# In the run of y's products, the second batch's first product is cut in two pieces, two columns at its old place and 128 columns at the end of the run

## The chip, the core and the metric

The kernel runs on one core of one Trainium2 chip. The core has a matrix engine (TensorE, PE in the profile, with its weight loads shown as PEld), a vector engine (VectorE, DVE), a scalar engine (ScalarE, ACT), a general engine (GpSimd, POOL), and queues that issue DMA transfers. The engines run side by side, each works through its own list of instructions in order, and they wait for each other by semaphores. The metric is the device time of one execution in microseconds, the lower the better.

## What is computed

Twelve layers of linear attention (there is no softmax) over a batch of 16 sequences of 256 tokens with 128 features, then a layer norm, a gated feed-forward block and another layer norm. The core of the reference, one layer with 16 heads of 8 features:

```python
for i in range(N_LAYER):
    qkv = x @ Wqkv[i].T + bqkv[i]
    q, k, v = jnp.split(qkv, 3, axis=-1)          # each (B, H, T, D) after a reshape
    att = jnp.einsum('bhqd,bhkd->bhqk', q, k) * scale
    y = jnp.einsum('bhqk,bhkd->bhqd', att, v)
    x = y @ Wproj[i].T + bproj[i] + x             # y with the heads side by side again
...
x = _layernorm(x0 + x)
h = jax.nn.silu(x @ wg.T) * (x @ wu.T)
x = _layernorm(x + h @ wd.T)
```

## The kernel before

Since nothing between the token vectors and the attention is nonlinear, the kernel doesn't carry tokens through the twelve layers. For each sequence it carries a matrix of 128 features by 130 columns (`tst`): the 128x128 map from the first tokens to the present ones, a column (number C = 128) for the share that all tokens have in common, and one column of padding. So W = C + 2 = 130. The tokens come in as a 128x128 Gram matrix of the first tokens for each sequence (`g0`). In each layer a sequence needs: q, k and v's maps from the state (`products`, L434 to L448), the Gram matrix times v (L455), the 8x8 blocks of k times that for each head (`mm_m` in `heads`, L499), these blocks times q (`mm_y`, L517, the run of y), and the projection with the sum into the state (`projection`, L534 to L541).

Sequences go in pairs (PB = 2, eight pairs p), and four pairs make a set (G = 4, two sets o). A call of `heads` treats one layer and one set: 8 sequences. The heads' blocks lie on the diagonal, so the 128x128 product falls into four groups of 32 features (four heads each), `group(g)`. TensorE's array is used there in tiles of 32 rows by 32 columns. In the run of y, the product of pair r, group g and sequence b takes rows `group(g)` of the weights `gm` and of q, and writes columns of the array `group(g + r)`, which are partitions of the output, into pair r's own bank of the accumulation memory, columns b W to (b + 1) W. So the 16 combinations of r and g use the 16 tiles of the array once each, all for the first sequence of the pairs (b = 0, the first batch); then all again for the second (b = 1). "First tile" is that of r = 0 and g = 0. There are 24 such runs (12 layers by 2 sets), each of 32 products. The data is fp32, and TensorE takes such a product in two passes with a weight load each: the profile shows 64 loads and 64 matmuls a run, not 32.

Behind the run of y, each pair's bank is rounded to the type fp32r (`yh`, on ACT or DVE by the copy helper, L205 or L207), DVE subtracts this from the bank to get the rest (`yl`, L530), and the projection multiplies both (L534 to L536: the low weights with yh, the high weights with yh and with yl). Pair r's projection waits for bank r alone. Its q is written by L444's matmuls, a copy (tile `qgv`) and a small addition to column C (L448); the first loads of the run of y wait for those.

The order of all work is settled when the program is built. Each `plan.op` has the estimated cost on each engine that could do it, what it reads and writes, and a priority; `Plan.run` places one operation after another, picks the engine that would end it first, and writes the instructions out in that order. A run of y is one operation with an estimate of 1200 ns on PE, whatever order its products have inside. TensorE's own list behind a run of y goes on with other pairs' products, which don't depend on it (L434 to L436, then L455), and reaches the projections about 2 us later.

The line at the core of the run, before:

```python
for b in range(PB):
    for r, p in enumerate(pairs):
        for g in range(G):
            nc.tensor.matmul(bank(pys[r])[group(g + r), b * W : (b + 1) * W], gm[group(g), r * PB + b, :], qss[p][group(g), b, :], start=True, stop=True)
```

Of the kernel before, what the change touches and what calls it, by code (L numbers as in the profile page):

```python
# [21 lines left out]
C = 128  # L22
# [3 lines left out]
PB = 2  # L26
NP = B // PB
W = C + 2
# [8 lines left out]
G = 4  # L37
# [141 lines left out]
def dve(n, fast=False):  # L179
    return 69 + n / (1.92 if fast else 0.96)  # L180


def pool(n):
    return 147 + 2.1 * n
# [7 lines left out]
def linear_attention_ffn_kernel(ctx: ExitStack, tc: tile.TileContext, x, xt, wall, wq0, bias, wg, wu, wd, out):  # L192
    nc = tc.nc
# [7 lines left out]
    bank = lambda v: banks[v.slot]  # L201
# [10 lines left out]
    def mul(e, dst, a, b):  # L212
        (nc.vector if e == DVE else nc.gpsimd).tensor_tensor(dst, a, b, ALU.mult)  # L213
# [104 lines left out]
    qss = [t[:, : PB * W].rearrange("p (a b) -> p a b", b=W) for t in qgvs]  # L318
# [52 lines left out]
    def offset_products(l, o):  # L371

        raw, pc = wts[l][0], Val("bank")
        c = tst[:, o * OB : (o + 1) * OB, C]

        def mm():
            for s in range(1 if l else 0, 3):
                for g in range(G):
                    cols = slice(32 * g, 32 * g + 32)
                    nc.tensor.matmul(bank(pc)[cols, s * OB : (s + 1) * OB], wraw[raw.slot][:, s * C : (s + 1) * C][:, cols], c, start=True, stop=True)  # L380
        return [raw, *vc[o * G : (o + 1) * G]], pc, mm

    def offsets(l, o, prio, pc):


        bs, ps = slice(o * OB, (o + 1) * OB), slice(o * G, (o + 1) * G)
        c = tst[:, bs, C]
        step = lambda costs, f, reads, writes: plan.op(costs, f, reads, writes, prio)
        src = lambda s: bank(pc)[:, s * OB : (s + 1) * OB]
        step({DVE: 133}, lambda e: nc.vector.tensor_scalar(vb[:, bs], src(2), bcol[:, l, 2:3], None, ALU.add), [pc, vbias], [vvc[o]])  # L390
        step({DVE: 133}, lambda e: nc.vector.tensor_scalar(kb[:, bs], src(1), bcol[:, l, 1:2], float(T), ALU.add, ALU.mult), [pc, vbias], [vkb[o]])
        if l == 0:
            step({DVE: 133}, lambda e: nc.vector.tensor_scalar(qc[:, bs], src(0), bcol[:, 0, 0:1], None, ALU.add), [pc, vbias], [vqc[o]])
        step({DVE: dve(32 * OB)}, lambda e: nc.vector.transpose(flat(vbb[:, bs]), vb[:, bs].unsqueeze(2).to_broadcast([128, OB, 32])), [vvc[o]], [vvb[o]])
        step({DVE: dve(32 * OB)}, lambda e: mul(e, kvo[:, bs], vbb[:, bs], kb[:, bs].unsqueeze(2).to_broadcast([128, OB, 32])), [vvb[o], vkb[o]], [vkvo[o]])

        if l < L - 1:
            def share(e):
                if e == ACT:
                    nc.scalar.activation(c, c, AF.Identity, bias=bcol[:, l, 3:4])  # L400
                else:
                    nc.gpsimd.tensor_scalar(c, c, bcol[:, l, 3:4], 0.0, ALU.add, ALU.add)
            step({POOL: 200, ACT: 220}, share, [vbias, *(vhi[ps] if l else [])], vc[ps])
# [68 lines left out]
    def first_offsets(o, prio):  # L472
        def fill(e):
            for p in range(o * G, (o + 1) * G):
                nc.gpsimd.tensor_copy(qss[p][:, :, C], qc[:, p * PB : (p + 1) * PB])
        plan.op({POOL: 600}, fill, [vqc[o]], vqo[o * G : (o + 1) * G], prio)

    def heads(l, o, prio, riders):

        raw = wts[l][0]
        pairs = range(o * G, (o + 1) * G)
        gm = gms[o]
        pm, pys = Val("bank"), [Val("bank") for _ in pairs]
        group = lambda g: slice(32 * (g % G), 32 * (g % G) + 32)
        src = [raw] if l == 0 else [vkv[p] for p in pairs]

        more = [(*r, *offset_products(*r)) for r in riders]

        def mm_m(e):
            for _, _, _, _, mm in more:
                mm()
            for p in pairs:
                for b in range(PB):
                    n = (p - o * G) * PB + b
                    tk = wraw[raw.slot][:, C : 2 * C] if l == 0 else kvs[p][:, b, 0, :]
                    for g in range(G):
                        nc.tensor.matmul(bank(pm)[group(g), n * 32 : n * 32 + 32], tk[:, group(g)], gvs[p][:, b, group(g)], start=True, stop=True)  # L499
        reads = [v for _, _, rs, _, _ in more for v in rs]  # L500
        if l == 0 and o == 1:

            reads += vw[:G]
        plan.op({PE: 890 + 140 * len(more)}, mm_m, [*(vgv[p] for p in pairs), *src, *reads], [pm, *(m[3] for m in more)], prio)
        for lo, oo, _, pc, _ in more:
            offsets(lo, oo, prio + (OFFSET if lo else 0), pc)
            if lo == 0:
                first_offsets(o, prio)
        plan.op({DVE: dve(OB * 32)}, lambda e: nc.vector.tensor_tensor(
            gm, bank(pm)[:, : OB * 32].rearrange("p (b j) -> p b j", j=32), kvo[:, o * OB : (o + 1) * OB], ALU.add), [pm, vkvo[o]], [vgm[o]], prio)  # L510
        plan.op({DVE: dve(OB * 32), POOL: pool(OB * 32)}, lambda e: mul(e, gm, gm, mask32.unsqueeze(1).to_broadcast([128, OB, 32])), [], [vgm[o]], prio)

        def mm_y(e):
            for b in range(PB):
                for r, p in enumerate(pairs):
                    for g in range(G):
                        nc.tensor.matmul(bank(pys[r])[group(g + r), b * W : (b + 1) * W], gm[group(g), r * PB + b, :], qss[p][group(g), b, :], start=True, stop=True)  # L517
        plan.op({PE: 1200}, mm_y, [vgm[o], *(vq[p] for p in pairs), *(vqo[p] for p in pairs)], pys, prio)
        return pys

# [231 lines left out]
    for l in range(L):  # L752
        if l + 1 < L:
            prep_weights(l + 1)
        for o in range(NO):
            at = l + OSTEP * o
            for p in range(o * G, (o + 1) * G):
                products(l, p, at)
            for r, py in enumerate(heads(l, o, at, [(l, o)] * (l < OWN) + [(l + o, 1 - o)] * (OWN <= l + o < L))):
                projection(l, o * G + r, py, at + (LSTEP * r if l == L - 1 else 0))  # L760
        if l < NP:
            center_tokens(l, l + 2)
# [38 lines left out]
```

## Time and profile before

| | |
|---|---|
| median of 3 runs | 305.56 us (304.95 to 306.38) |
| the profiled execution | 305.16 us, of which the span is 303.2 us |
| instructions | 12834 |
| granted TensorE clock | 0.998 of full speed |
| TensorE matmuls busy | 294.3 us (97% of the span) |
| TensorE weight loads busy | 269.8 us (89%) |
| DVE, ACT, POOL busy | 226.1, 217.7, 137.8 us |
| y's matmuls (L517) | 1536, 280 ns mean, 25.8 us together |
| y's weight loads | 1536, 103 ns mean, 17.2 us together |

The span is the time from the first to the last instruction that the profiler recorded; the difference to the execution's own time lies before and behind it. Durations of instructions on one engine can overlap, so that a sum of means is not time: 64 matmuls of 280 ns of one run of y stand in 1.07 us. Starts are what counts there. A line such as "102.98 1.07 PE L517 MATMUL ... x64" of the timeline gives the start in the span, the time covered, the engine, the line of the kernel, what is done and how often. In a bracket behind it stands how long the engine was idle before, and what ended the wait. "Issue" there means that the profile shows nothing that was waited for.

### The profile page before, as it was taken

The page shows a single profiled execution, that of the slowest core. Times are in us where ns is not written, and L with a number is a line of the kernel's source. Part 1 is how long each engine was busy: PE and PEld are TensorE (multiplying, and loading weights), DVE is VectorE, ACT ScalarE, POOL GpSimd, SP SyncE. Part 2 cuts the span into 40 slices and gives each one's busy share as a digit, 9 for nine tenths or more (in the row PEclk, how much of TensorE's full clock was granted, in tenths as well). Part 3 has the DMA queues.
Part 4 walks back from the last instruction along what each step waited for, and adds up shares of the span by engine and source line. Part 5 has one row for each costly group of instructions (what it writes and reads, how often), then busy time and mean ns, then how long its engine had stood idle before and what let it go on. Part 6 is the DMA issues. An engine that isn't in the chain of part 4 may idle for free.

```text
span 303.2 us, 12834 instructions
## 1 busy us (share of the span) xinstructions
PE 294.3 (97%) x5376; PEld 269.8 (89%) x5376; DVE 226.1 (75%) x683; ACT 217.7 (72%) x559; POOL 137.8 (45%) x208
## 2 busy tenths in 40 slices
PE   8999999999999999999999999999999999999981
PEld 8989999999999999999999999989999998878760
DVE  4796887777677676876767777786644789999993
ACT  3556877867777768777686666777887558788875
POOL 8256452334531445225432354224431167777883
PEclk9999999999999999999999999999999999999999
DMA  7624213112031120311302102120000000000225
GB/s 214 163 91 131 67 39 89 38 46 82 3 89 37 39 89 4 88 40 28 98 2 56 37 17 50 49 68 17 2 2 4 3 1 2 0 0 8 63 70 138
DMA packets 22489, 15.65 MB, mean 52 GB/s; under 512 B 1952, under 2 KB 19872, under 8 KB 22432
## 3 DMA queue, kind: packets, MB, share of 16 engines
q1 hardware_dynamic: 21872, 14.62, 17.3%
q8 instruction: 42, 0.69, 0.9%
q10 hardware_dynamic: 560, 0.22, 0.3%
q14 instruction: 15, 0.12, 0.1%
HBM read 8.02 MB, written 2.10 MB: 33 GB/s over the span
## 4 chain that ended last, share of the span: by engine, by line
PE 87%; DVE 10%; issue 1%; ACT 1%; POOLq 0%; POOL 0%; DVEq 0%
PE bank L455 14%; PE bank L434 8%; PE bank L517 8%; PE bank L436 7%; PE bank L435 7%; PE bank L442 5%; PE bank L499 5%; PE bank L536 4%; PE bank L534 4%; PE bank L535 4%; PE bank L443 3%; PE bank L444 3%; PE bank L336 3%; DVE st L618 2%; PE bank L706 2%; PE bank L707 2%
## 5 line engine op out<-in xcount | busy, mean ns | idle before, releaser
L210 POOL TENSOR_TENSOR thl<-tst,thl 128x260 fp32r<-128x260 f32 x88 | 64.8, 768 | 123.1 <-ACT thl L205 123.1
L205 ACT COPY qgv<-bank 128x256 f32<-128x256 f32 x169 | 59.8, 378 | 19.2 <-PE bank L444 12.9
L205 ACT COPY kv<-bank 128x512 f32<-128x512 f32 (+1 forms) x93 | 53.4, 575 | 19.5 <-PE bank L436 14.2
L434 PE MATMUL bank<-whl,thl 128*128 128x256 f32 x176 | 51.9, 295 | 0.0
L436 PE MATMUL bank<-whl,thl 128*128 128x256 f32 x176 | 49.7, 282 | 0.0
L435 PE MATMUL bank<-whl,thl 128*128 128x256 f32 x176 | 49.4, 281 | 0.0
L455 PE MATMUL bank<-kv,g 128*128 128x128 f32 x352 | 46.1, 275 | 0.0
L541 DVE TENSOR_TENSOR tst<-bank,tst 128x260 f32<-128x260 f32 x96 | 36.9, 425 | 9.4 <-PE bank L536 9.0
L205 ACT CAST thl<-tst 128x260 fp32r<-128x260 f32 x88 | 33.0, 408 | 14.6 <-DVE tst L541 14.5
L455 PEld LDWEIGHTS bank<-kv,g 128*128 128x128 f32 x352 | 42.7, 191 | 0.4 <-issue 0.4
L448 DVE TENSOR_SCALAR qgv<-bank,bcol 128x2 f32<-128x2 f32 x88 | 19.2, 221 | 28.3 <-ACT qgv L205 22.9
L434 PEld LDWEIGHTS bank<-whl,thl 128*128 128x128 f32 x176 | 33.1, 188 | 4.0 <-issue 3.8
L530 DVE TENSOR_TENSOR yhl<-bank,yhl 128x260 fp32r<-128x260 f32 x96 | 34.4, 420 | 2.2 <-ACT yhl L205 2.1
L436 PEld LDWEIGHTS bank<-whl,thl 128*128 128x128 f32 x176 | 33.1, 188 | 0.3 <-POOL thl L210 0.2
L435 PEld LDWEIGHTS bank<-whl,thl 128*128 128x128 f32 x176 | 33.2, 189 | 0.0
L442 PE MATMUL bank<-thl,whl 128*128 128x260 f32 x88 | 28.8, 327 | 0.0
L205 ACT CAST yhl<-bank 128x260 fp32r<-128x260 f32 (+1 forms) x61 | 21.8, 408 | 8.3 <-PE bank L517 7.7
L207 DVE CAST yhl<-bank 128x260 fp32r<-128x260 f32 (+1 forms) x43 | 16.7, 430 | 12.7 <-PE bank L517 12.7
L517 PE MATMUL bank<-qgv,gm 32*32 32x130 f32 x1536 | 25.8, 280 | 0.2 <-DVE gm L213 0.2
L443 PE MATMUL bank<-thl,whl 128*128 128x260 f32 x88 | 24.8, 282 | 0.0
L444 PE MATMUL bank<-thl,whl 128*128 128x260 f32 x88 | 24.7, 281 | 0.0
L517 PEld LDWEIGHTS bank<-qgv,gm 32*32 32x32 f32 x1536 | 17.2, 103 | 5.5 <-ACT kv L205 0.3
(157 smaller groups left out, 694.7 us busy)
## 6 DMA issues: line engine op xcount, KB each, us to landing
wraw<-wall SPq DMA_DIRECT2D x12, 256.0 KB, 3.0
wpt<-whl SPq DMA_DIRECT2D x24, 96.0 KB, 2.2
qgv<-x SPq DMA_DIRECT2D x8, 256.0 KB, 5.0
xt<-xt SPq DMA_DIRECT2D x8, 256.0 KB, 3.1
out<-kv SPq DMA_DIRECT2D x7, 256.0 KB, 2.3
wpt<-whl SPq DMA_DIRECT2D x24, 64.0 KB, 2.7
wpt<-whl SPq DMA_DIRECT2D x24, 32.0 KB, 1.9
wraw<-wg SPq DMA_DIRECT2D x1, 192.0 KB, 3.2
```

The costliest lines, as they stand in the source:

```text
L205: nc.scalar.copy(dst, src)
L210: (nc.vector if e == DVE else nc.gpsimd).tensor_tensor(dst, a, b, ALU.subtract)
L434: nc.tensor.matmul(o, hi[:, b, 0:C], hl(0, 1, 2), start=True, stop=False)
L435: nc.tensor.matmul(o, hi[:, b, 0:C], hl(1, 1, 2), start=False, stop=False)
L436: nc.tensor.matmul(o, lo[:, b, 0:C], hl(0, 1, 2), start=False, stop=True)
L442: nc.tensor.matmul(o, hl(0, 0), flat(hi), start=True, stop=False)
L443: nc.tensor.matmul(o, hl(0, 0), flat(lo), start=False, stop=False)
L444: nc.tensor.matmul(o, hl(1, 0), flat(hi), start=False, stop=True)
L455: nc.tensor.matmul(bank(pgv)[:, b * C : (b + 1) * C], g0[p][:, b, :], tv(b), start=True, stop=True)
L517: nc.tensor.matmul(bank(pys[r])[group(g + r), b * W : (b + 1) * W], gm[group(g), r * PB + b, :], qss[p][group(g), b, :], start=True, stop= ...
L530: plan.op({DVE: dve(PB * W)}, lambda e: nc.vector.tensor_tensor(yl, bank(py)[:, : PB * W], yh.bitcast(F32), ALU.subtract), [py, vyh[p]], [ ...
L541: plan.op({DVE: dve(PB * W)}, lambda e: nc.vector.tensor_tensor(ts, bank(pw)[:, : PB * W], ts, ALU.add), [pw], [vt[p], vc[p]], prio)
```

## The change

The first batch's 16 products stay as they are. Of the second batch, the first tile's product (r = 0, g = 0) is cut along the columns that stream through the array: its last two columns, 128 and 129, are done at its old place, between the two batches, and its columns 0 to 127 behind the fifteen other products, as the last thing of the run. Both pieces use the same weights, which are loaded for each. A run has 33 products then in place of 32, and the last writer of pair 0's bank is the last product of the run. Nothing else is changed; the operation's estimated cost is the same.

```diff
+        tiles = [(r, g) for r in range(G) for g in range(G)]
+        order = [(0, r, g, 0, W) for r, g in tiles]
+        for b in range(1, PB):
+            order += [(b, 0, 0, C, W), *((b, r, g, 0, W) for r, g in tiles[1:]), (b, 0, 0, 0, C)]
+
         def mm_y(e):
-            for b in range(PB):
-                for r, p in enumerate(pairs):
-                    for g in range(G):
-                        nc.tensor.matmul(bank(pys[r])[group(g + r), b * W : (b + 1) * W], gm[group(g), r * PB + b, :], qss[p][group(g), b, :], start=True, stop=True)
+            for b, r, g, lo, hi in order:
+                nc.tensor.matmul(bank(pys[r])[group(g + r), b * W + lo : b * W + hi], gm[group(g), r * PB + b, :], qss[pairs[r]][group(g), b, lo:hi], start=True, stop=True)
         plan.op({PE: 1200}, mm_y, [vgm[o], *(vq[p] for p in pairs), *(vqo[p] for p in pairs)], pys, prio)
```

## The prediction

> **What bounds the kernel now.** I read the page first: its engine rows, the slices, then the chain of the work that ended last.
>
> ```profile
> PE 294.3 (97%) x5376; PEld 269.8 (89%) x5376; DVE 226.1 (75%) x683; ACT 217.7 (72%) x559; POOL 137.8 (45%) x208
> ...
> PEclk9999999999999999999999999999999999999999
> ...
> PE 87%; DVE 10%; issue 1%; ACT 1%; POOLq 0%; POOL 0%; DVEq 0%
> ```
>
> TensorE is busy for 97% of the span at its full clock (0.998 granted), and 87% of the chain is TensorE's. So a nanosecond more or less in a y run is a nanosecond of the end, if TensorE does not wait for data just behind it. Next I read the chain in order of time around one y run, and the weight loads there:
>
> ```profile
> 103.05 1.00 PE bank L517 x56
> ...
> 102.97 0.80 PEld L517 LDWEIGHTS bank<-qgv,gm 32*32 32x32 f32 x64
> 103.98 0.19 PEld L434 LDWEIGHTS bank<-whl,thl 128*128 128x128 f32 x1 [0.20 <-issue]
> ```
>
> The reader is to see that the y run stands whole on the chain, with 0.20 us behind its last matmul in which the array changes from 32x32 tiles to 128x128. One product is four records: two weight loads and two passes, 64 of each in a run. There are 24 runs. Then I cut the run into stretches (columns: us, PE busy, PEld busy with their counts, clock, DMA):
>
> ```profile
> 102.97:103.22 0.25, 0.24 (x32) 0.24 (x33) 1.00 0.00 0
> 103.22:103.29 0.07, 0.07 (x32) 0.00 (x0) 1.00 0.40 110
> 103.29:103.41 0.12, 0.12 (x30) 0.10 (x1) 1.00 0.86 213
> 103.41:103.78 0.37, 0.37 (x42) 0.36 (x30) 1.00 0.69 176
> 103.78:103.98 0.20, 0.20 (x25) 0.00 (x0) 1.00 0.15 36
> ```
>
> This is the place the change touches. The first batch loads its 32 weights and the first one of the second batch (33), then nothing is loaded for 0.07 us, then one weight in 0.12 us, then 30 in 0.37 us. Start by start in the trace, from the run's first load (102.97): first passes of batch one at 2 to 102 ns, one each 6.7 ns; second passes at 137 to 237; the second batch's first product passes at 322 and 433; its second product loads at 437; from there one product each 16.6 ns, to a last pass at 807; the next load, L434's, at 1004. The second batch's first product therefore seems to hold up the other fifteen.
>
> **What holds it.** The question is whether that product is held by its own length (the tile streams 130 columns twice, and pass two cannot start before pass one is through: 322 + 108 = 430), or by something that doesn't depend on it. The trace has a second case: the runs of m (L499, behind L380's), whose passes are short, so that no tile is busy for long. There too, products come fast at first, and then on a grid of 16.6 ns. What sets the start of this grid is the same to a nanosecond in all: it is the recorded end of the second pass of the run's very first product, plus 30 to 31 ns. In the usual y run that pass starts at 137 and lasts 269, to 406, and the load of the 18th product is at 437. In the runs of m behind L380 it ends at 230 and the load is at 260. In the one m run that stands alone, at 233 us, it ends at 251 and the load is at 282. The 17th product's first pass obeys it too: the first product's first pass ends at 295, the 17th's starts 27 later, at 322; its second pass starts 27 after 406, at 433. In the y run at 200.6 us, whose first product came late, the same ends are 298 and 409, and the starts 324 and 435. So it looks as if 16 products (64 records) may be open, and the 17th gets in record by record as the first one ends. This is my reading of these rows; it says that the 17th product's length is not what the others wait for.
>
> **The change part by part.** Removed: the 17th product as one of 130 columns. Put in its place: two columns of it, four records again. By the reading above they get in when the first batch's first product ends, as now: passes at 322 and 433, next load at 437. Gain: nothing. The bounds: at worst nothing is lost, since the records are as many; at best the two passes follow each other at the nearest short row. In the m runs behind L380, passes of 8 and of 32 columns on one tile follow each other at 31 to 32 ns alike, so 433 would be 353: 80 ns a run, 24 x 80 = 1.9 us. I take nothing, because the m runs, whose passes are short, are held to the same end.
>
> Added: at the end, four records on the tile of row 0 and column 0, 128 columns. That tile's load is free from 237 on, and rows and columns of tiles go on in the order that the run had. On the grid it costs one step: 16.6 ns (its passes would start at about 690 and 823). The last pass streams 128 columns in place of 130, less by 2 x 108/130 = 1.7 ns, before the 197 ns from the last pass to L434's load. Net: +15 ns a run, 24 x 15 = +0.36 us. Bounds: with the step hidden altogether, -1.7 x 24 = -0.04 us. If the piece were to run alone, as the 17th product does now (322 to 441), 119 - 1.7 = 117 ns, 24 x 117 = +2.8 us. I take the grid, whose fifteen steps stand directly ahead of it and include changes of row, column and bank.
>
> [...] The trace puts a whole product, two loads and two passes, on 16.6 ns here, so its row goes into the sum.
>
> Moved: the signal that bank 0 is ready. At present the four banks of the run are announced at 0.89, 0.98, 1.08 and 1.17 us from its start, 92 ns apart. Bank 0's last writer goes from the 20th product of the run to the very end, behind bank 3's; by the same spacing its signal comes at about 1.19, some 0.3 us later. ACT (in some runs DVE) has the rounding of that bank to yhl first in its queue and the next banks' behind it. What covers it, by the timelines of ACT, DVE and TensorE:
>
> ```profile
> 103.89 0.66 ACT L205 CAST yhl<-bank 128x260 fp32r<-128x260 f32 x2 [0.22 <-PE bank L517]
> 105.01 0.59 ACT L205 COPY kv<-bank 128x512 f32<-128x512 f32 x1 [0.47 <-PE bank L436]
> ...
> 104.66 1.42 DVE L530 TENSOR_TENSOR yhl<-bank,yhl 128x260 fp32r<-128x260 f32 x4
> 106.59 0.43 DVE L541 TENSOR_TENSOR tst<-bank,tst 128x260 f32<-128x260 f32 x1 [0.50 <-PE bank L536]
> ...
> 105.88 0.36 PE L534 MATMUL bank<-yhl,whl 128*128 128x260 f32 x1
> ...
> 106.20 0.28 PE L536 MATMUL bank<-yhl,whl 128*128 128x260 f32 x1
> ```
>
> ACT's two roundings move 0.3 us into the 0.47 us in which it idles for L436. DVE's first subtraction (L530, 104.66) is behind DVE's own roundings, and TensorE needs its result at 106.20, 1.1 us after its end at 105.08. In the runs where DVE rounds banks 0 and 1, the four subtractions come 0.3 us later and 0.9 us are left. The thin places are the first run (0.05 us at L536, but DVE's own roundings set it, not bank 0's) and the last two, with 0.56 and 0.40 us. Priced at nothing; if that cover were gone in these three, 3 x 0.3 = +0.9 us. What is late next in that case is L536 of the first projection. The order of the operations, their engines and all DMA queues stay as they are: the planner's costs are untouched. The waits on q's copies stand on the first batch's loads and cover both batches.
>
> Sum: the profiled execution took 305.16 (span 303.2, 1.96 around it), which becomes 305.52. It lies 0.40 under the median of 305.56; against that the forecast is 305.56 + 0.36 = 305.9.
>
> **Rivals.** First, the 17th product's own length is what holds the others. For it: 322 + 108 is 430, as near to 433 as the other reading's sum. Against it: the m runs. The time: -80 + 15 = -65 ns a run, -1.6 us, 304.0 (beyond 0.5% by a hair). Second, slower: the last piece runs alone at the end of each run, its passes one after the other with nothing beside them, 117 ns a run, 308.4. For it: the run's other product on this tile that has an open stretch to itself took 111 between its passes. Against it: the grid lets the first passes of products run ahead of earlier second passes. It decides from 64 ns a run, where 24 runs make 1.53 us (0.5%). Third, the late bank 0 reaches TensorE at the thin places: 305.9 + 0.9 = 306.8.
>
> **How the numbers follow.** A measurement of this kernel tells about 0.5% (1.5 us) from no change. Forecast 72%, its own range 305.2 to 306.7 from the spread of the runs shown (-0.6 to +0.8 around the median). First rival 10%, two thirds of it beyond 0.5%; second 9%; third 9%, a small part of it beyond. Faster 7%, within 0.5% 83%, slower 10%. The range takes in the forecast, the third rival and the near edge of the first: 304.5 to 306.9.
>
> **What would show it.** In the profile after: 66 loads and 66 passes in each y run; passes of the two-column piece at about 322 and 433; the next load at 437; the last pass near 823, L434's load near 1019; bank 0's rounding 0.3 us later and no new wait at L534 and L536. I am wrong if the two-column passes stand 30 ns apart and the next load comes well ahead of 437, or if the last product's passes are followed by a longer pause than 197 ns.

## The result, and the profile after

The changed kernel takes 306.48 us (median of 20 runs, 305.38 to 307.64) against 305.59 us for the kernel before (20 runs, 304.77 to 307.35). The ratio is 1.003, with a 95% interval of 1.0016 to 1.0044: 0.5 to 1.35 us slower, around 0.9. That lies inside the range that was given (304.5 to 306.9) and within the 0.5% that was called the likeliest. The amount was put at 0.36 us, below the interval's lower end.

The page of the changed kernel, in the lines that were shown of before, and two of its list of DMA queues that are needed further on (packets, MB, share of 16 engines):

```profile
PE 295.2 (97%) x5424; PEld 270.5 (89%) x5424; DVE 226.5 (74%) x683; ACT 217.4 (71%) x559; POOL 137.7 (45%) x208
...
PEclk9999999999999999999999999999999999999998
...
q8 instruction: 42, 0.69, 1.0%
q14 instruction: 14, 0.11, 0.1%
...
PE 87%; DVE 10%; issue 1%; ACT 1%; POOLq 0%; POOL 0%; DVEq 0%
```

There are 48 loads and 48 passes more (two of each in 24 runs), TensorE is busy 0.9 us longer, and its share of the chain is what it was. The bound has not moved to another engine. The span is 304.1 us (303.2 before).

The chain in order of time, around the same run of y (start, us, what):

```profile
103.84 1.02 PE bank L522 x53
104.86 0.32 PE bank L434
```

The weight loads there (start, us, line and operation, how many, idle before):

```profile
103.77 0.82 PEld L522 LDWEIGHTS bank<-qgv,gm 32*32 32x32 f32 x66
104.79 0.19 PEld L434 LDWEIGHTS bank<-whl,thl 128*128 128x128 f32 x1 [0.20 <-issue]
```

And the run cut into stretches at the same offsets as before (stretch, us, PE busy with its count, PEld busy with its count, clock, DMA share, GB/s):

```profile
103.77:104.02 0.25, 0.25 (x32) 0.24 (x33) 1.00 0.00 0
104.02:104.09 0.07, 0.07 (x32) 0.00 (x0) 1.00 0.39 110
104.09:104.21 0.12, 0.12 (x30) 0.10 (x2) 1.00 0.83 205
104.21:104.59 0.38, 0.38 (x43) 0.38 (x32) 1.00 0.86 217
104.59:104.79 0.20, 0.20 (x26) 0.00 (x0) 1.00 0.15 36
```

The reader is to see that the pattern has not changed. The first batch loads its 32 weights and the first of the second batch, then nothing for 0.07 us, then two weights in 0.12 us, then 32. Start by start from the run's first load: the two-column passes at 323 and 434, the next load at 438, the last pass at 823, L434's load at 1019 (1004 before). It is 1018 or 1019 in 19 of the 24 runs. The 20th run, whose first product comes late, takes 1037, against 1023 before: the same step. The forecast had 322, 433, 437, 823 and 1019.

Bank 0's rounding and what hangs on it, by the timeline of ACT:

```profile
104.95 0.65 ACT L205 CAST yhl<-bank 128x260 fp32r<-128x260 f32 x2 [0.49 <-PE bank L522]
105.81 0.59 ACT L205 COPY kv<-bank 128x512 f32<-128x512 f32 x1 [0.20 <-PE bank L436]
```

and by that of DVE:

```profile
105.43 1.42 DVE L535 TENSOR_TENSOR yhl<-bank,yhl 128x260 fp32r<-128x260 f32 x4
107.40 0.43 DVE L546 TENSOR_TENSOR tst<-bank,tst 128x260 f32<-128x260 f32 x1 [0.55 <-PE bank L541]
```

The rounding starts 1.18 us behind the run's first load (0.92 before; bank 0's signal was put at 1.19), and ACT's idle time ahead of L436's copy has shrunk from 0.47 to 0.20 us, as foretold. L539 and L541 (L534 and L536 of before) show no new wait in any run. One thing about the signals was not foreseen: TensorE raises its semaphore three times at the end of a run of y, at 0.96, 1.12 and 1.16 us, where it did so four times before (0.89, 0.98, 1.08, 1.17). In three of the 24 runs it does so once.

So the run of y does what was forecast, within about a nanosecond, in 20 runs of 24. The other four hold the rest. The longest of them, by the weight loads and by the chain:

```profile
83.76 0.72 PEld L522 LDWEIGHTS bank<-qgv,gm 32*32 32x32 f32 x55
84.94 0.17 PEld L522 LDWEIGHTS bank<-qgv,gm 32*32 32x32 f32 x11 [0.46 <-issue]
85.30 0.19 PEld L434 LDWEIGHTS bank<-whl,thl 128*128 128x128 f32 x1 [0.20 <-issue]
```

```profile
83.83 0.92 PE bank L522 x47
84.75 0.19 issue
84.94 0.43 PE bank L522 x11
```

Behind its 55th load this run, the eighth, stands still: 0.46 us without a load, of which 0.19 us is seen on the chain as a time in which TensorE had nothing to do and waited for nothing that the profile names. Its next load of L434 comes at 1545 ns in place of 1019. The others are the 11th run (1083), the 14th (1066) and the 12th (1027). Summed over the 24 runs, the time from the first load to L434's load is 988 ns more than before: 360 ns of added steps (24 x 15) and 628 ns of such holds. Not all of it stays to the end: between the runs of y the profile gains 0.33 us, which is taken up below.

**What stands at the holds.** I counted TensorE's records (loads, passes and its semaphore records) from the start of its list. The load at which a hold ends is number 3521 in this run, and 4801 and 6082 in the 11th and 14th: the remainder against 256 is 193 or 194. The queue q8 above carries 42 packets of 16 KB; 42 x 256 = 10752 is the number of TensorE's loads and passes in the kernel before, and in `eight` below it carries 45 for 11520, which is 45 x 256. So I put a packet at 256 records. The hold ends 1.34 to 1.50 us behind the end of such a transfer: in the eighth run the transfer lasts from 82.14 to 83.47, and the load comes at 84.94. In the kernel before, the smallest distance from a transfer's end to the load at this place is 1.32 us, in the 16th run, with no hold. So it looks as if TensorE ran out of instructions: the next block of its list had not become usable yet. That is my reading of these rows; what they show is the remainder and, in this run, 0.46 us without a load. Four more records a run move all later boundaries (28 records by the eighth run), and some fall late into a run of y, where the kernel before starts 128 records in 0.81 us, against 3.6 us in the mean of its list (10752 in 303.2 us).

### The profile page after: what moved, and what is told of

Its sections match the earlier page's. It is cut to its first block, busy times and chain, and to the rows that moved or that the text cites. A ratio compares the mean times of both kernels' runs of the same rounds, so it can differ in the third digit from the quotient of the medians.

```text
span 304.1 us, 12908 instructions
## 1 busy us (share of the span) xinstructions
PE 295.2 (97%) x5424; PEld 270.5 (89%) x5424; DVE 226.5 (74%) x683; ACT 217.4 (71%) x559; POOL 137.7 (45%) x208
## 4 chain that ended last, share of the span: by engine, by line
PE 87%; DVE 10%; issue 1%; ACT 1%; POOLq 0%; POOL 0%; DVEq 0%
PE bank L455 14%; PE bank L522 8%; PE bank L434 8%; PE bank L436 7%; PE bank L435 7%; PE bank L442 5%; PE bank L499 5%; PE bank L539 4%; PE bank L541 4%; PE bank L540 4%; PE bank L444 3%; PE bank L443 3%; PE bank L336 3%; DVE st L623 2%; PE bank L711 2%; PE bank L712 2%
## 5 line engine op out<-in xcount | busy, mean ns | idle before, releaser
L434 PE MATMUL bank<-whl,thl 128*128 128x256 f32 x176 | 51.8, 294 | 0.0
L436 PE MATMUL bank<-whl,thl 128*128 128x256 f32 x176 | 49.4, 281 | 0.0
L434 PEld LDWEIGHTS bank<-whl,thl 128*128 128x128 f32 x176 | 33.1, 188 | 3.9 <-issue 3.8
L436 PEld LDWEIGHTS bank<-whl,thl 128*128 128x128 f32 x176 | 33.1, 188 | 0.3 <-POOL thl L210 0.2
L522 PE MATMUL bank<-qgv,gm 32*32 32x130 f32 (+2 forms) x1584 | 26.6, 277 | 0.4 <-issue 0.2
```

Of the source, the lines that this page charges most:

```text
L434: nc.tensor.matmul(o, hi[:, b, 0:C], hl(0, 1, 2), start=True, stop=False)
L436: nc.tensor.matmul(o, lo[:, b, 0:C], hl(0, 1, 2), start=False, stop=True)
L522: nc.tensor.matmul(bank(pys[r])[group(g + r), b * W + lo : b * W + hi], gm[group(g), r * PB + b, :], qss[pairs[r]][group(g), b, lo:hi], st ...
```

## The experiments

Two theories of the 0.9 us were tried against each other. The first is that of the prediction with the holds added: 0.36 us of steps, and what the shifted instruction list costs. The second is the prediction's third rival in a wider form: the moved last writer of bank 0 costs something somewhere. Ahead of the experiments the reading of the queue (16 products open, the 17th gets in as the first ends) was open as well. All edits below are against the changed kernel unless it is said otherwise. In the table, the run's length is the time from the first load of a run of y to L434's load, in the middle one of 24 runs; "steps" and "held" divide what the 24 runs of one profile sum to above those of the kernel before: the middle run's excess 24 times, and the rest. What is held need not be held at a boundary of the list.

| kernel | ratio, 95% interval | run, ns | steps, ns | held, ns |
|---|---|---|---|---|
| changed | 1.0030 [1.0016, 1.0044] | 1019 | 360 | 628 |
| again | 1.0029 [1.0016, 1.0043] | 1019 | 360 | 960 |
| whole_last | 1.0002 [0.9989, 1.0015] | 1005 | 21 | 0 |
| swap | 1.0023 [1.0007, 1.0039] | 1005 | 24 | 934 |
| in_place | 1.0013 [1.0000, 1.0027] | 1021 | 408 | 224 |
| first_short | 1.0035 [1.0019, 1.0051] | 1009 | 120 | 215 |
| eight | 1.0110 [1.0086, 1.0133] | 1135 | 3144 | 269 |
| before_s28 | 1.0018 [1.0003, 1.0032] | 1004 | 0 | 11 |
| before_s28_2 | 1.0008 [0.9996, 1.0019] | 1004 | 0 | 0 |
| swap_s44 | 0.9997 [0.9981, 1.0013] | 1005 | 8 | 0 |
| whole_last_s28 | 1.0009 [0.9992, 1.0026] | 1004 | 0 | 305 |
| after_s44 | 1.0031 [1.0018, 1.0045] | 1017 | 312 | 50 |
| after_s44_2 | 1.0033 [1.0020, 1.0045] | 1017 | 312 | 98 |

**again.** The changed kernel without an edit, for a second profile.

> The changed kernel once more, nothing edited. Three theories of its +0.9 us. The step: the added product costs one step of 16.6 ns less 1.7, 24 runs make +0.36 us, ratio 1.0012, and what goes beyond is not the change's. Held supply: with four more records a run, TensorE's list of instructions falls otherwise into the pieces in which it is fetched, and single runs are held in the middle; in the profile after, the run at 83.8 us is held 0.53 us, and three others 0.12 us together. Then the hold comes back at the same run, and the ratio is again near 1.003. Accident: holds come in each execution at other places or not at all; then this profile has them elsewhere or has none, and over many executions the ratio goes toward 1.001.

The middle run is 1019 again, and the eighth run is held at the same load:

```profile
83.56 0.72 PEld L522 LDWEIGHTS bank<-qgv,gm 32*32 32x32 f32 x55
84.69 0.17 PEld L522 LDWEIGHTS bank<-qgv,gm 32*32 32x32 f32 x11 [0.41 <-issue]
```

The 11th run is held longer than in the first profile (1371 against 1083), the 14th too (1111). In the fifth, load 2241, again with remainder 193, is held by 0.05 us without making the run longer. So these places belong to the program, and the length of a hold differs from one execution to another. The 18th run (1076) is held as well, at load 7773, whose remainder is 93. It is held at the same number in `in_place` (1130), and by 0.05 us in after_s44 and after_s44_2 at 7817, the same load of the program with the list 44 records longer ahead of it. That hold doesn't go with the blocks of the list, and nothing here shows what makes it; the fourth run of `eight` (1267, remainder 178) has another.

**whole_last.** The product is not cut, but done whole at the end of the run.

```diff
-            order += [(b, 0, 0, C, W), *((b, r, g, 0, W) for r, g in tiles[1:]), (b, 0, 0, 0, C)]
+            order += [*((b, r, g, 0, W) for r, g in tiles[1:]), (b, 0, 0, 0, W)]
```

> The second batch's first product isn't cut but goes whole to the end of the run (32 products, the moved signal of bank 0 stays). The step: nothing is added, so the run is as long as before (last pass at 807, next load at 1004) and the ratio 1.000 (0.999 to 1.001); the product that is now the 17th is another one of 130 columns, and its passes are at 322 and 433 too. Were the late signal of bank 0 what costs, this kernel would keep the whole +0.9 us, 1.003. Held supply: as many records as before, so 1.000.

```profile
102.60 0.80 PEld L522 LDWEIGHTS bank<-qgv,gm 32*32 32x32 f32 x64
103.60 0.19 PEld L434 LDWEIGHTS bank<-whl,thl 128*128 128x128 f32 x1 [0.20 <-issue]
```

With 64 loads the run takes 1005, nothing is held, and the time is that of before (1.0002). Bank 0's signal is late here as in the changed kernel, and the run raises three signals as there. So the lateness by itself doesn't bring the 0.9 us (the interval leaves it 0.46 at most). The 17th place is taken by another tile's product of 130 columns, and its passes start at 322 and 433 as ever. With the two-column piece's 323 and 434 this shows that neither the length nor the tile of the 17th product sets them.

**swap.** The pieces change places: 128 columns at the old place, two at the end.

```diff
-            order += [(b, 0, 0, C, W), *((b, r, g, 0, W) for r, g in tiles[1:]), (b, 0, 0, 0, C)]
+            order += [(b, 0, 0, 0, C), *((b, r, g, 0, W) for r, g in tiles[1:]), (b, 0, 0, C, W)]
```

> The two pieces change places: 128 columns as the 17th product, two columns at the end. As many products and records as in the changed kernel. The step: the last piece streams so briefly (passes near 690 and 746) that the 32nd product's second pass, at 807, still ends last; the next load is at 1004 as before, and the ratio is 1.000. If a product costs its 16.6 ns wherever it stands and whatever it streams, the next load is at 1020 and the ratio 1.0013. Held supply: as many instructions as in the changed kernel, so 1.002 to 1.003, with runs held in the middle.

```profile
83.42 0.72 PEld L522 LDWEIGHTS bank<-qgv,gm 32*32 32x32 f32 x55
84.62 0.17 PEld L522 LDWEIGHTS bank<-qgv,gm 32*32 32x32 f32 x11 [0.48 <-issue]
...
103.41 0.82 PEld L522 LDWEIGHTS bank<-qgv,gm 32*32 32x32 f32 x66
104.41 0.19 PEld L434 LDWEIGHTS bank<-whl,thl 128*128 128x128 f32 x1 [0.18 <-issue]
```

With a last piece of two columns the run needs 1005 although it has 66 loads (1019 with a last piece of 128, also at 66): the step is hidden. The holds stand all the same (the eighth run 1553, the 11th 1396), and in this profile they are nearly all that its runs of y lose.

**in_place.** The cut alone, without moving the large piece.

```diff
-            order += [(b, 0, 0, C, W), *((b, r, g, 0, W) for r, g in tiles[1:]), (b, 0, 0, 0, C)]
+            order += [(b, 0, 0, C, W), (b, 0, 0, 0, C), *((b, r, g, 0, W) for r, g in tiles[1:])]
```

> The cut alone, without the move: two columns as the 17th product, the 128 others as the 18th, ahead of the other tiles'. Bank 0 is signalled at its old place. The step: one product more of 16.6 ns, the last one a whole one, so the next load is at 1021 and 24 runs make +0.40 us. Held supply: the list stands as in the changed kernel, so the eighth, 11th and 14th runs are held again, 0.5 to 1 us together. Both: ratio near 1.003. If the late signal of bank 0 were part of the price, this kernel would be faster than the changed one, near 1.001.

```profile
103.03 0.82 PEld L522 LDWEIGHTS bank<-qgv,gm 32*32 32x32 f32 x66
104.06 0.19 PEld L434 LDWEIGHTS bank<-whl,thl 128*128 128x128 f32 x1 [0.20 <-issue]
```

The step is a full 16.6 ns: the run takes 1021, where the last product still streams 130 columns, against 1019 with a last piece of 128. The holds are 224 ns in this profile, and the time is 1.0013 where 1.003 was expected with holds of 0.5 to 1 us. The expectation had also named 1.001 as the sign that the late signal is part of the price, and the time lies there; its interval overlaps the changed kernel's, so this is not settled.

The eighth run is held by 15 ns at the same load. What differs is the moment at which the 16 KB transfer of that block ends: 0.76 us ahead of the run's first load here, but 0.27 to 0.30 us ahead in the changed kernel, `again` and `swap`, which are held by 526, 471 and 548 ns, and 0.40 in `first_short` (108 ns). The transfer's length is a part of this (1.08 us here, 1.33 to 1.40 there, where an 8 KB packet of another instruction queue, q14, runs at the same time), but not the whole: ahead of the 11th run it took 0.88 us in `again` and `swap`, started late, ended 0.43 and 0.41 us ahead, and the run was held by 352 and 391 ns. In the changed kernel it ended 0.76 ahead of that run, and the hold was 64 ns. What sets the moment at which a transfer starts isn't shown.

**first_short.** The first batch's first product is cut in place of the second batch's, so that the run's very first product is short.

```diff
-        order = [(0, r, g, 0, W) for r, g in tiles]
+        order = [(0, 0, 0, C, W), *((0, r, g, 0, W) for r, g in tiles[1:])]
...
-            order += [(b, 0, 0, C, W), *((b, r, g, 0, W) for r, g in tiles[1:]), (b, 0, 0, 0, C)]
+            order += [*((b, r, g, 0, W) for r, g in tiles), (0, 0, 0, 0, C)]
```

> The first batch's first product is cut instead of the second's: two columns as the very first product of the run, its other 128 columns as the last one. This tests what sets the 17th product's start. By the reading that 16 products may be open, and the 17th gets in as the first one ends: the first product's passes are at 2 and about 33, its end at about 192, so the 17th's first pass comes at about 190 in place of 322 and its second at about 298, when its tile is through; the 18th product's second pass still waits for the second product's end (412) and gets in at about 439, so the grid begins at 443 for the 19th in place of 437 for the 18th, the 33rd loads at about 675 and the last pass is at about 810, the next load near 1006: ratio 1.000 to 1.001. If the 17th's start hangs on something else (the array's change of mode, a fixed time from the run's start), it stays at 322 and 433, the run is as long as the changed kernel's, 1018, and the ratio 1.001 to 1.003.

The stretches of one run (columns as above, run from 104.56):

```profile
104.56:104.81 0.25, 0.25 (x33) 0.25 (x34) 1.00 0.00 0
104.81:104.89 0.08, 0.08 (x33) 0.08 (x2) 1.00 0.35 96
104.89:105.01 0.12, 0.12 (x30) 0.11 (x3) 1.00 0.81 205
105.01:105.37 0.36, 0.36 (x42) 0.36 (x30) 1.00 0.71 184
```

Two weights are loaded in the stretch in which the kernel before loads none. The first product's passes end at 188 and 220 ns; the 17th's first pass starts at 216 (188 + 28) in place of 322, and the 18th's load at 251 (220 + 31) in place of 437. So the reading of the queue holds in a case made to test it: the 17th and 18th come 28 and 31 ns behind the ends of the first product's passes. The times foreseen were 190 and 298 for the 17th's passes, against 216 and 326, because the first product's second pass was put at 33 and started at 54. The 18th product is no better off: its own passes start at 329 and 440, 28 ns behind the ends of the second product's, which is as long as ever. The next ones follow on the old grid, and the last pass comes at 812. So the run takes 1009. The time, 1.0035, is more than these 120 ns of steps and 215 ns of holds make. In its profile the stretch from the first run of y to the second is 0.92 us longer than in the kernel before, as DVE waited for a part of a weight transfer that came late:

```profile
20.19 0.72 DVE L207 CAST whl<-wraw 128x512 fp32r<-128x512 f32 x1 [0.82 <-DMA wraw<-wall]
```

That this is so in most executions isn't shown. Part of its time lies outside the span, as is told below.

**eight.** Eight tiles are cut in the same way: 40 products a run.

```diff
-            order += [(b, 0, 0, C, W), *((b, r, g, 0, W) for r, g in tiles[1:]), (b, 0, 0, 0, C)]
+            order += [*((b, r, g, C, W) for r, g in tiles[:8]), *((b, r, g, 0, W) for r, g in tiles[8:]), *((b, r, g, 0, C) for r, g in tiles[:8])]
```

> The cut done to eight tiles: the second batch begins with eight pieces of two columns (pairs 0 and 1), then eight whole products, then the eight pieces of 128 columns; 40 products a run. The step: eight steps of 16.6 ns less 1.7, so the last pass stands near 940 and the next load near 1135, 131 ns more than before, 24 runs make +3.1 us. The passes of the 17th stay at 322 and 433 with eight short products in a row. Held supply adds 0 to 1.5 us, by where the list falls. Ratio 1.010 to 1.015. [...]

```profile
105.10 0.94 PEld L522 LDWEIGHTS bank<-qgv,gm 32*32 32x32 f32 x80
106.24 0.19 PEld L434 LDWEIGHTS bank<-whl,thl 128*128 128x128 f32 x1 [0.20 <-issue]
```

The run is 1135: 8 x 16.6 - 1.7 = 131 ns more than 1004. An added product of this kind costs one grid step each, for one (15 ns) as for eight (131).

**The instruction list moved by itself.** The next six have idle matmuls at the very start of the kernel, ahead of any work, which shift TensorE's list by 28 or 44 records; they are narrower, and all of them together last about as long as the 30 of before (52 of them 3.41 us in after_s44_2, those 30 3.38). 28 is the shift that the changed kernel has by its eighth run. With 44 the held places fall 44 records earlier into these runs (behind 66 in place of 110 records of the eighth), and their transfers end 2.3 to 3.1 us ahead of the eighth, 11th and 14th runs. Their edit, with 44 and 86 columns for a shift of 28, or 52 and 74 columns for one of 44:

```diff
-WARM = 30
+WARM = 44
...
-        nc.tensor.matmul(banks[7][:, :128], zero, zero, start=True, stop=True)
+        nc.tensor.matmul(banks[7][:64, :86], zero[:, :64], zero[:, :86], start=True, stop=True)
```

**before_s28** is the kernel before with the shift of 28.

> [...] In the profiles of the changed kernel and of the exchanged pieces each hold lies at a record whose number is 192 to 194 beyond a multiple of 256; in the eighth run that is behind 110 of its records. Held supply, as the place in the list: the eighth run, near 83.5 us, is held here too, by 0.4 to 0.6 us, though nothing was added to it, and the ratio is 1.001 to 1.002. If the holds come from the added records or the pieces themselves, no run is held, all next loads stand at 1004, and the ratio is 1.000.

The eighth run of y by its weight loads:

```profile
83.47 0.81 PEld L517 LDWEIGHTS bank<-qgv,gm 32*32 32x32 f32 x64
84.48 0.19 PEld L434 LDWEIGHTS bank<-whl,thl 128*128 128x128 f32 x1 [0.20 <-issue]
```

There is a hold at the load foreseen, the 55th, but of 9 ns, not 400 to 600. The transfer of that block ended 0.82 us ahead of the run. The expectation was wrong in size: the shift sets where a hold can be (the 55th load of this run), and how long it is goes with the moment at which the transfer ends (9 ns at 0.82 us ahead here, 526 at 0.29 in the changed kernel). The time is up all the same (1.0018).

**swap_s44** is `swap` with the shift of 44.

> The exchanged pieces (128 columns as the 17th product, two at the end), with TensorE's list put 44 records later by 52 narrow idle matmuls (64x74) at the start. By count, the places 193 beyond a multiple of 256 then fall behind 85, 101 and 106 records of three runs of y (the 14th, 17th and 20th); the kernel before has them behind 105, 106 and 110 in three of its runs, and the changed one behind 101, with no hold there. Held supply, as the place in the list: no run is held by more than 0.1 us, the next loads stand at 1005, and the ratio is 1.000 (0.999 to 1.001) in place of 1.0023. If the holds come from the 33rd product itself, runs 8 and 11 are held again and the ratio stays at 1.002.

Every run of y is 1003 to 1005 (the 20th 1024, as it was 1023 before), no hold is left, and the ratio falls from 1.0023 to 0.9997, as expected. The intervals of the two overlap, and it will be seen below that a good part of the difference lies outside the span, where no hold can be: this run agrees with the theory, but doesn't carry it.

**whole_last_s28** is `whole_last`, which had no hold and no loss, with the shift of 28.

> The uncut product moved whole to the end of the run (32 products, late signal of bank 0), with TensorE's list 28 records later by 44 narrow idle matmuls, so that the place 193 beyond a multiple of 256 falls behind 110 records of the eighth run of y. The kernel before, put as late, was held there by 9 ns only: the 16 KB transfer of instructions that the hold waits for took 1.05 us there, and 1.34 to 1.40 us in the four kernels that signal bank 0 late and are held longer, where an 8 KB transfer of instructions falls into it. If it is the late signal that brings these two transfers together, the eighth run is held here by 0.4 to 0.6 us although no product was added, and the ratio is 1.001 to 1.002. If the late signal has no part in it, the hold stays under 0.1 us and the ratio is near 1.000 to 1.001.

```profile
84.17 0.72 PEld L522 LDWEIGHTS bank<-qgv,gm 32*32 32x32 f32 x55
85.09 0.16 PEld L522 LDWEIGHTS bank<-qgv,gm 32*32 32x32 f32 x9 [0.21 <-issue]
```

Now the eighth run is held at its 55th load, for 0.28 us, with 64 loads and no added product. So a hold needs no added product. But the position in the list alone doesn't make it either: before_s28 and before_s28_2 have the same position and were held there by 9 and 3 ns. Here the transfer started 1.40 us ahead of the run and ended 0.39 ahead; there it started 1.87 and 1.63 ahead and ended 0.82 and 0.67 ahead. The expectation gave the late signal a part in this, by bringing the two transfers together. They do meet here, but the 16 KB transfer took 1.01 us, not 1.34 to 1.40: it came late, not long. The hold is below the 0.4 to 0.6 us foreseen, and in the time (1.0009) it is not to be told from nothing.

**after_s44** is the changed kernel with the shift of 44.

> The changed kernel with TensorE's list put 44 records later by 52 narrow idle matmuls at the start, as was done to the kernel with the exchanged pieces. If the place in the list makes the holds, no run is held by more than 0.1 us, the step of 14 to 15 ns a run stays (next loads at 1018 to 1019), and the ratio is 1.0012 (1.000 to 1.0025) in place of 1.0029. If the holds come with the 128-column piece at the end, they are back near 84 and 114 us and the ratio is 1.003.

No run is held at a boundary of the list any more (the 50 ns left are nearly all the 18th run's), and the time is as long as ever: 1.0031. This expectation failed. Its profile had the late part of a weight transfer that `first_short` showed, and the stretch behind the first run of y was 0.90 us longer:

```profile
19.44 0.75 DVE L207 CAST whl<-wraw 128x512 fp32r<-128x512 f32 x1 [0.81 <-DMA wraw<-wall]
```

**after_s44_2** and **before_s28_2** repeat two of these kernels without an edit, to see whether that late part was the cause, and what the shift does to the kernel before.

> The changed kernel with its list 44 records later once more, nothing edited. In its first profile no run of y was held by more than 0.05 us, but one of the sixteen parts of a weight load landed at 19.4 us where the others had landed by 17.9, DVE waited 0.8 us for it, and TensorE lost 0.76 us behind the first run of y. If that is an accident, it is gone in this profile, the span is the one before plus 0.35 to 0.5 us, and the ratio is about 1.0013. If the shifted list brings it about, it is there again, and the ratio is again 1.003.

> The kernel before with its list 28 records later once more. Its first profile had the hold of the eighth run at the place foreseen, but with 9 ns, in an execution of 305.13 us, while the median of its 12 executions was 306.23. If the length of the hold varies between executions and the profile fell on a short one, this profile may show 0.1 to 0.5 us there, and the ratio is again 1.001 to 1.002. If the hold is always that short, it is under 0.05 us again and the ratio falls to 1.000.

The eighth run of after_s44_2:

```profile
84.46 0.82 PEld L522 LDWEIGHTS bank<-qgv,gm 32*32 32x32 f32 x66
85.48 0.19 PEld L434 LDWEIGHTS bank<-whl,thl 128*128 128x128 f32 x1 [0.20 <-issue]
```

No late part this time, 98 ns of holds, none of them at a boundary, and again 1.0033. So the late part isn't what keeps the shifted kernel slow. before_s28_2 has a hold of 3 ns and 1.0008.

**Where the time of all executions lies.** Each run has a span beside its time, so the two can be told apart over all runs, not the profiled ones alone (differences of means against the kernel before of the same comparison, 95% intervals by resampling the runs; for the changed kernel against all 104 runs of the kernel before). The changed kernel's span is 0.66 us longer (0.42 to 0.93), `again`'s 0.65 (0.38 to 0.89). Of that 0.36 are steps, and 0.3 is left (0.06 to 0.57).

What lies outside the span is longer by 0.14 us in the changed kernel (0.10 to 0.18, medians), and it is longer in `whole_last` too (0.10), but hardly in `in_place` (0.06, -0.01 to 0.12) and not in before_s28 (0.04, -0.05 to 0.11). So it seems to go with the product at the run's end, not with the cut. The changed kernel and `whole_last` have 22 semaphore instructions fewer than before (19 of ACT's, 3 of DVE's), and TensorE raises its semaphore 30 times less; why their time outside the span is longer, nothing here shows. In some executions it is longer by much more: 4 of 20 of the changed kernel, 5 of 12 of `swap` and 4 of 12 of `first_short` have 2.6 to 3.5 us outside the span, where the kernel before has 1.96 in the middle and never 2.5 in 104. In means this makes 0.33 us for the changed kernel, 0.52 and 0.51 for the other two. `again`, the same kernel as the changed one, has none.

**What lies between the runs of y.** From the first load behind a run to the first load of the next (behind the last run, to the end of the span), the profile of the changed kernel is shorter than that of before, mostly by 7 to 15 ns at a time, 0.33 us in all. So its span, 0.88 us longer, is made of 0.22 us by which the first run starts later, 0.99 in the runs, and -0.33 between them. `whole_last`, which has no step to give back, gains 0.18 in the same way, `again` 0.21 and `in_place` 0.24. In the six kernels with a shifted list the sum lies between -0.04 and +0.14, the late parts left aside. What makes these stretches shorter isn't shown. But the shift takes away more than the holds: from the first run on, the changed kernel's profile loses 0.66 us and `again`'s 1.11, after_s44_2's 0.40.

`swap` warns against reading one profile as the mean: its profile has 934 ns of holds, but its spans are only 0.18 us longer (-0.15 to 0.50), and 0.43 (0.12 to 0.80, medians) lies outside them; swap_s44 has -0.15 and 0.15. Of the 0.6 us between the two, as much lies outside the span as in it.

The narrow idle matmuls may have a price of their own: in the kernel before the two runs with them have spans longer by 0.41 (0.06 to 0.74) and 0.20 (-0.13 to 0.51), with 9 and 3 ns held. That would explain why after_s44 stays where it is: 0.36 of steps, 0.05 of holds and 0.2 to 0.4 of idle matmuls are 0.6 to 0.8, against 0.75 measured in its spans. But swap_s44 has the same idle matmuls and a span of -0.15 (-0.54 to 0.25). So this is an argument, not a finding.

## Why the prediction was right, and where it was off

**What bounds the kernel: right.** TensorE's share of the chain is 87% before and after, and the middle run of y lengthened by what its own starts show.

**The front piece gains nothing: right, and for the reason given.** The two-column passes start at 323 and 434, 111 ns apart as those of 130 columns did, and the next load at 438. The better case (80 ns gained, two passes 31 ns apart) did not come about; the starts fit a second pass that waits for the end of the run's first product (406 + 28 = 434). `whole_last` shows the same starts with a long product in the 17th place, and `first_short` moves them (to 216 and 326) by shortening the first product.

**The added product costs one grid step less 1.7 ns: right.** 15 ns a run, in the changed kernel; 16.6 where the last piece keeps its 130 columns (`in_place`); 131 for eight (`eight`). The records of the runs of m before, 176 ns for a pass of 8 columns and 196 for one of 32, make the 108 ns for 130 columns, on which the 1.7 rests, an estimate of 130 x 20/24.

**The late signal of bank 0 is covered: right.** ACT's idle time ahead of L436's copy took it (0.47 us before, 0.20 after), and `whole_last` prices it at 1.0002, together with the signal that is gone from each run. A part of 0.1 us outside the span was neither seen nor looked for.

**The rivals.** The 17th product's own length holds the others: refuted by 438. The last piece runs alone for 117 ns: refuted by 1019, and by `eight`. The late bank 0 reaches TensorE at the thin places: refuted by the missing waits at L539 and L541, and by `whole_last`.

**The step that failed** is the sum, "24 x 15 = +0.36 us": it took 24 runs for 24 equal runs, and a product for the time that it takes on the array. It left out that four records more a run also move every later record in the instruction list, and that in this kernel a run of y can be held in its middle (0.46 us without a load in the eighth). In two profiles of the changed kernel this term is 0.63 and 0.96 us, nearly all of it at boundaries of the list; over all executions the spans leave 0.3 (0.06 to 0.57) for it and for anything else inside the span. Outside the span 0.14 more lies in medians, and 0.33 in means. In means 0.36 + 0.3 + 0.33 is the whole 0.99 by which the times differ, but the last two terms are measured, not explained. The trace of before could have warned: 1.32 us lie there between the end of a transfer of q8 and the load at the boundary, in a run that is not held, and no hold was seen to end earlier than 1.16 us behind a transfer.

That 306.48 lies inside the range is due to the range's width. Its upper end came from the spread of the runs and from the third rival, which did not come about; no term in it stood for what was really added.

**What stays open.** The holds, their places and their lengths are shown in the traces, and that one arises without an added product where the boundary of a block falls late into a run (`whole_last_s28`) and the transfer ends late (0.39 us ahead of it there). That they are the whole of the unforeseen part of the measured time is not shown: the changed kernel with its holds moved away kept its 1.003 twice. Nor is it shown why a transfer starts late, what shortens the stretches between the runs, or what lengthens the time outside the span.

No kernel here beats the one before; `whole_last` and swap_s44 can't be told from it.

## What to carry to other kernels

In a dense run of short products on a tiled array, count what a change adds as grid steps of that run (16.6 ns each here), and look at what is first and last in it: here a short piece in the middle gained nothing (its passes at 323 and 434, a whole product's at 322 and 433), while a short last one cost nothing (`swap`: 1005 against 1004). Then look at TensorE's instruction list as a queue like any other (42 transfers of 16 KB here, and holds of up to 0.55 us): find the boundaries of its blocks, the transfers that bring them, and how much time lies between, before calling an edit of a few instructions free. And where a result is a few tenths of a per cent, compare spans and what lies outside them over all executions; one profile's holds can be several times what the mean span shows (0.93 against 0.18 us in `swap`).

## What the runs showed of the hardware that was not expected

- TensorE can stand still in the middle of a dense run, as if it were short of instructions. The long holds stand at records whose number leaves 193 or 194 against 256, last up to 0.55 us, and end 1.16 to 1.50 us behind the end of the 16 KB transfer. How long they are goes with the moment at which that transfer ends: 0.27 to 0.43 us ahead of the run for those of 0.1 to 0.55 us in the eighth and 11th runs, 0.67 to 0.86 ahead for those under 0.07. Shorter holds, up to 0.13 us, stand at a few other records too, for no reason that is shown.
- The starts fit a reading by which sixteen products of four records each can be open. The next gets in record by record as the oldest ends: its pass 26 to 28 ns behind the oldest product's passes, the next load 30 to 32 ns behind its last, in the runs of y and m that were taken apart and in `first_short`.
- The moment at which the full clock is granted differs between executions, from 4.1 to 6.8 us into the span in the fourteen profiles (4.92 before, 5.39 in the changed kernel; up to there L336's matmuls start 0.21 to 0.35 us apart, then 0.11), and the first run of y moves with it, from 18.0 to 19.2 us (18.34 and 18.56 in these two). This is as large as the whole effect of the change, so spans of single profiles say little about it.
- A part of a weight transfer of the first layer landed late in `first_short`, swap_s44 and after_s44 (19.4 us against 17.9 in after_s44) and cost DVE some 0.8 us there. The late part was not there when after_s44 was repeated.
